# Attention's products with v in four 64x64 quarters of the array

## The chip, the cores and the metric

The kernel is one program on one NeuronCore of a Trainium2 chip. The core has five engines that run beside each other, each with its own queue of instructions: TensorE (matrix products, in the profile PE, and its weight loads, PEld), VectorE (DVE), ScalarE (ACT), GpSimd (POOL) and SyncE (SP, which here mostly issues DMAs). TensorE multiplies a stationary operand, loaded by a weight load, with a moving operand that streams through an array of 128 rows (the contraction, on the partitions of SBUF) and 128 columns (the output's partitions), and writes its result to PSUM, 128 partitions by eight banks of 512 f32. VectorE and ScalarE read PSUM; the next product into a bank waits until they have.

The metric is the device time of one execution in microseconds. The time before is 3694.07 us, the median of three runs (3691.95 to 3695.59).

## The reference, cut to what matters

The reference is a chain of four layers on an image of 48 x 48 positions with 768 channels in f32: a transformer block with global attention, a Fourier mixer, a scan with rotations and depthwise convolutions, and a second Fourier mixer. Only the attention of the first layer is touched by the change:

```python
attn = jnp.einsum('bqc,bkc->bqk', q * scale, k)
...
attn = (attn.reshape(B * nh, H, W, H, W) + rel_h[:, :, :, :, None] + rel_w[:, :, :, None, :]).reshape(B * nh, H * W, H * W)
attn = jax.nn.softmax(attn, axis=-1)
out = jnp.einsum('bqk,bkc->bqc', attn, v)
```

There are 12 heads of 64 channels and 2304 positions. For each head and each query, the scores against all 2304 keys get two position terms, go through the softmax, and weight the rows of v.

## The kernel before

The kernel runs the layers one after another, in stages: normalised input, q, k, v and the position terms (to DRAM); attention; projection; the two-layer perceptron; the first Fourier mixer; the scan; the second mixer. All products are f32, apart from the position terms added to the scores, which are one-pass f32r.

Attention (`attention_bounded`, from line 586) takes the heads in six pairs (`pr`), and each pair's queries in five chunks (`qc`) of 464 columns, the last of 448. A chunk `c = (pr, qc)` goes through the 18 tiles of 128 keys (`kt`), three in a step (`KB = 3`): 6 x 5 x 6 = 180 steps. The two heads of a pair are called `s` = 0 and 1; head `s` has its channels in partitions `64 s` to `64 s + 63`.

For one key tile:

- `products` (line 617) multiplies keys with queries. The contraction is over 64 channels, so head 0 uses the upper 64 rows of the array and head 1 the lower 64, with 128 columns each (the keys). Their results go to two different PSUM banks of one tile `s`; the pool `ps_s` holds three such pairs of banks.
- `scores` (line 626) adds the position terms to the same banks with a one-hot product of 64 rows by 128 columns for each head (line 633), ScalarE takes the exponential of both heads in one instruction into an SBUF tile `p` (line 635), and VectorE adds `p` to an accumulator `acc`, from the second key tile on (lines 640 and 643). No maximum is subtracted: a bound that the first stage computes allows it, and otherwise `attention_any` is run, which the change does not touch.
- `values` (line 647) multiplies v with `p`. The contraction is over the tile's 128 keys, so all 128 rows are used, and each head's 64 channels take one half of the array's columns: 128 rows by 64 columns, the outputs of both heads in the two halves of the partitions of one bank, `av`. It collects over the 18 key tiles.

At the end of a chunk `row_sums` (line 656) multiplies `acc` with a block of ones in the same way, which gives each head's sum over all keys, spread over its 64 partitions, in a bank `rs`; VectorE takes the reciprocal from there. `finish` (line 667) multiplies `av` with it into `oT`, the attention's output in SBUF. `av` and `rs` have one bank each (the pool `ps_v`), so with the six of `ps_s` all eight banks are taken.

The steps overlap by one: in step `i`, `products` and `scores` of step `i` are written first, then `row_sums` (if a chunk ends), `values` and `finish` of step `i - 1`. So at the end of a chunk, the first three key tiles of the next chunk stand on TensorE ahead of the row sums and of the last three products with v, and another three key tiles stand between those and the next chunk's first product into `av`.

Each engine runs its queue in order. The order in a queue is that of the program's text as a priority, but the framework's planner, which simulates the program with its own costs when it is compiled, may put an instruction ahead of another that it expects to be ready later. In the profile the reciprocal (line 664) runs on VectorE ahead of the add of key tile 2 of the next chunk (line 643), which the text has before it.

Beside these, SyncE loads the next keys, values, queries and position terms; GpSimd prepares weights for later stages; and in the first chunk twelve groups of position terms are still computed (`last_terms_w`, line 208: four products of 128 rows by 96 columns each, line 203, then a copy on ScalarE and two subtracts on VectorE). Their PSUM tile has the tag `rs`, too (line 674).

Of the kernel before, what the change touches and what calls it, by code (L numbers as in the profile page):

```python
# [12 lines left out]
F32 = mybir.dt.float32  # L13
F32R = mybir.dt.float32r
AF = mybir.ActivationFunctionType
ALU = mybir.AluOpType
# [4 lines left out]
P = 128  # L21
# [4 lines left out]
NT = T // P  # L26
NH, HD = 12, 64
# [523 lines left out]
def queries(qc):  # L551

    return slice(qc * QB, min(T, (qc + 1) * QB))
# [32 lines left out]
def attention_bounded(tc, ahead, oT, last_terms, beside, load_next):  # L586

    nc = tc.nc  # L600
    KB = 3
    (load_keys_values, load_chunk, load_terms), kvs, qbs, bts, ones, oneh = ahead
    with (
        tc.tile_pool(name="at_p", bufs=10) as pp,
        tc.tile_pool(name="at_r", bufs=2) as rp,
        tc.tile_pool(name="at_o", bufs=2) as op,
        tc.tile_pool(name="at_ps", bufs=3, space=PSUM) as ps_s,
        tc.tile_pool(name="at_pv", bufs=1, space=PSUM) as ps_v,
    ):
        keys = [kv[:, :T] for kv in kvs]  # L610
        vals = [kv[:, T:].rearrange("p (t c) -> p t c", t=NT) for kv in kvs]

        probs, scs = {}, {}
        size = lambda c: queries(c[1]).stop - queries(c[1]).start
        held = lambda c: qbs[(c[0] * NQB + c[1]) % 2]

        def products(c, kt):
            pr, qc = c
            n = size(c)
            ps = ps_s.tile([P, 2, 512], F32, tag="s", name=f"s_{pr}_{qc}_{kt}")  # L620
            for s in range(2):
                rows = slice(s * HD, (s + 1) * HD)
                nc.tensor.matmul(ps[:, s, :n], lhsT=keys[pr % 2][rows, kt * P : (kt + 1) * P], rhs=held(c)[rows, :n], start=True, stop=False)  # L623
            scs[c, kt] = ps

        def scores(c, kt):
            pr, qc = c
            n = size(c)
            b, j = divmod(kt, KJ)
            ps = scs.pop((c, kt))  # L630
            for s in range(2):
                rows = slice(s * HD, s * HD + NBR)
                nc.tensor.matmul(ps[:, s, :n], lhsT=oneh[rows, b % 2, :], rhs=bts[b // 2][rows, j, :n], start=False, stop=True)  # L633
            p = pp.tile([P, 2, QB], F32, tag="p", name=f"p_{pr}_{qc}_{kt}")[:, :, :n]
            nc.scalar.activation(p, ps[:, :, :n], AF.Exp)  # L635
            probs[c, kt] = p

            if kt == 1:
                acc = rp.tile([P, 2, QB], F32, tag="acc", name=f"acc_{pr}_{qc}")[:, :, :n]
                nc.vector.tensor_tensor(acc, probs[c, 0], p, ALU.add)  # L640
                probs[c] = acc
            elif kt > 1:
                nc.vector.tensor_tensor(probs[c], probs[c], p, ALU.add)  # L643

        avs, recs = {}, {}

        def values(c, kt):
            pr, qc = c
            if kt == 0:
                avs[c] = ps_v.tile([P, 512], F32, tag="av", name=f"av_{pr}_{qc}")  # L650
            p = probs.pop((c, kt))
            for s in range(2):
                rows = slice(s * HD, (s + 1) * HD)
                nc.tensor.matmul(avs[c][rows, : size(c)], lhsT=vals[pr % 2][:, kt, rows], rhs=p[:, s, :], start=kt == 0, stop=kt == NT - 1)  # L654

        def row_sums(c):
            pr, qc = c
            n = size(c)
            acc = probs.pop(c)
            rs = ps_v.tile([P, 512], F32, tag="rs", name=f"rs_{pr}_{qc}")  # L660
            for s in range(2):
                nc.tensor.matmul(rs[s * HD : (s + 1) * HD, :n], lhsT=ones, rhs=acc[:, s, :], start=True, stop=True)
            rec = rp.tile([P, QB], F32, tag="rec", name=f"rec_{pr}_{qc}")[:, :n]
            nc.vector.reciprocal(rec, rs[:, :n])
            recs[c] = rec

        def finish(c):
            pr, qc = c
            av, rec = avs.pop(c), recs.pop(c)
            nc.vector.tensor_tensor(oT[:, pr, queries(qc)], av[:, : size(c)], rec, ALU.mult)  # L670

        work = [((pr, qc), k0) for pr in range(NC) for qc in range(NQB) for k0 in range(0, NT, KB)]
        other = beside(op, lambda name: pp.tile([P, 2, QB], F32, tag="p", name=name).rearrange("p a c -> p (a c)")[:, : 2 * TB].rearrange("p (a c) -> p a c", a=2))
        terms = last_terms(rp, lambda name: ps_v.tile([P, 512], F32, tag="rs", name=name))
        other_at = {15 + 28 * n // 5 for n in range(29)}

        def next_terms(c, g):
            if c in sequence:
                load_terms(bts[g], c, g)

        sequence = [(pr, qc) for pr in range(NC) for qc in range(NQB)]
        after = dict(zip(sequence, sequence[1:]))

        mid, end = {2, 3, 4, 5, 7, 8, 9, 10, 11, 13}, {8, 10}
        for i in range(len(work) + 1):
            if i in other_at:
                next(other, None)
            if i == 0:
                next(terms)
            if i == len(work) - 8:  # L690
                load_next()
            if i < len(work):
                c, k0 = work[i]
                pr, qc = c
                nxt = (pr, qc + 1) if qc + 1 < NQB else (pr + 1, 0)
                if k0 == 0 and nxt[0] < NC:
                    load_chunk(held(nxt), nxt)
                if k0 == 0 and c != (0, 0):
                    next_terms(c, NG3 - 1)
                elif k0 in (6, 12):  # L700
                    next_terms(after.get(c), k0 // 6 - 1)
                if k0 == 0 and qc == (1 if pr else 3) and pr + 1 < NC:
                    load_keys_values(kvs[(pr + 1) % 2], pr + 1)
                for kt in range(k0, k0 + KB):
                    products(c, kt)
                    scores(c, kt)
            if i in mid:
                next(terms)
            if i:
                c, k0 = work[i - 1]  # L710
                if k0 + KB == NT:
                    row_sums(c)
                for kt in range(k0, k0 + KB):
                    values(c, kt)
            if i in end:
                next(terms)
            if i:
                if k0 + KB == NT:
                    finish(c)
        for _ in itertools.chain(terms, other):  # L720
            pass
# [663 lines left out]
def block_kernel(ctx: ExitStack, tc: tile.TileContext, a: dict):  # L1385
# [58 lines left out]
    with tc.If(bounded > 0) as which:  # L1444
        attention_bounded(tc, ahead, oT, last_terms, beside, load_pw)
# [489 lines left out]
```

## Time and profile before

| | |
|---|---|
| median of the runs | 3694.07 us |
| profiled execution | 3694.35 us, span 3692.6 us, mean granted clock 0.986 |
| attention | about 494 to 1552 us of the span |
| L654, products with v | 2160 matmul instructions, mean 558 ns each, busy 456.5 us together |
| L623, keys with queries | 2160, mean 566 ns |
| L633, position terms | 1080, mean 729 ns |
| L635, exponential (ScalarE) | 540, mean 940 ns |
| L643, accumulator (VectorE) | 480, mean 1177 ns |
| L664, reciprocal (VectorE) | 30, 3050 ns in the middle |
| L670, output (VectorE) | 30, 627 ns in the middle |

PE is TensorE's matmuls and PEld its weight loads. Matmuls that run beside each other in parts of the array, or that follow each other in its pipeline, overlap in the records, so the mean length of a record is longer than its share of the time; distances between starts say more. Within one line of an answer, "x12" are twelve instructions merged; a bracket at the end of a line is the idle time of the engine ahead of it and what ended that. Shapes of matmuls are given as rows*columns of the weights, and then the moving operand.

### The profile page before, as it was taken

The numbers are of one execution on the slowest core, as the hardware profiler recorded it, in microseconds if no ns is written. First come the engines' busy times: TensorE is split into PE (matmuls) and PEld (weight loads), VectorE is DVE, ScalarE is ACT, GpSimd is POOL, SyncE is SP. The second block draws the span as 40 slices with busy tenths as digits, with TensorE's granted clock in tenths as the row PEclk, the third lists the DMA queues.
The fourth block names the chain that finished last, engine by engine and source line by source line (L and its number), as shares of the span: only waits on it lengthen the run. The fifth ranks groups of instructions, "written<-read, shape, count | busy, mean of one in ns | idle before, by whom it ended". The sixth has DMA issues, their size and how long they took to land.

```text
span 3692.6 us, 52195 instructions
## 1 busy us (share of the span) xinstructions
PE 3592.4 (97%) x20914; PEld 2182.6 (59%) x20914; DVE 1995.3 (54%) x3011; ACT 1140.1 (31%) x1731; POOL 666.3 (18%) x498
## 2 busy tenths in 40 slices
PE   7999989999999999999999999999999998999998
PEld 4666554444444444455555555555568867995685
DVE  6544346666666666655334323232345478994445
ACT  1222134444444444303201210121023265223341
POOL 4010001111111111051000000000023303981131
PEclk9999999999999999999999999999999999999999
DMA  7666764746554543344335433533544302112345
GB/s 254 209 219 191 220 191 127 203 125 160 140 145 118 147 121 102 88 141 157 104 122 171 128 105 121 165 105 107 155 134 111 97 20 101 37 30 83 99 121 154
DMA packets 267738, 491.82 MB, mean 133 GB/s; under 512 B 37182, under 2 KB 220286, under 8 KB 261280
## 3 DMA queue, kind: packets, MB, share of 16 engines
q1 hardware_dynamic: 257680, 467.45, 43.0%
q10 hardware_dynamic: 9808, 20.94, 1.6%
q8 instruction: 168, 2.75, 0.3%
q14 instruction: 82, 0.67, 0.1%
HBM read 344.69 MB, written 143.62 MB: 132 GB/s over the span
## 4 chain that ended last, share of the span: by engine, by line
PE 76%; DVE 3%; POOL 2%; DMA 2%; ACT 1%; issue 1%; ACTq 0%; SPq 0%; DVEq 0%; POOLq 0%
PE p L960 13%; PE p L1023 13%; PE s L623 12%; PE av L654 12%; PE c L1187 4%; PE s L633 3%; PE pj L169 3%; PE f_z L1594 2%; PE f_z L1595 2%; PE f_x L1559 2%; PE so L1365 2%; PE f_u L1609 2%; POOL t L1288 1%; DVE s L1300 1%; DVE H L1284 1%
## 5 line engine op out<-in xcount | busy, mean ns | idle before, releaser
L643 DVE TENSOR_TENSOR acc<-acc,p 128x928 f32<-128x928 f32 (+1 forms) x480 | 565.2, 1177 | 255.2 <-ACT p L635 222.4
L635 ACT ACTIVATE p<-s 128x928 f32<-128x928 f32 (+1 forms) x540 | 506.7, 940 | 522.8 <-PE s L633 501.2
L623 PE MATMUL s<-qt,kv 64*128 64x464 f32 (+1 forms) x2160 | 529.2, 566 | 4.9 <-DMA qt<-q_d 4.9
L1023 PE MATMUL p<-w,h 128*128 128x384 f32 x1512 | 492.7, 486 | 0.0
L654 PE MATMUL av<-p,kv 128*64 128x464 f32 (+1 forms) x2160 | 456.5, 558 | 0.0
L1023 PEld LDWEIGHTS p<-w,h 128*128 128x128 f32 x1512 | 286.2, 190 | 196.9
L633 PE MATMUL s<-bt,oneh 64*128 64x464 f32 (+1 forms) x1080 | 399.1, 729 | 0.9 <-DMA bt<-rh_d 0.9
L623 PEld LDWEIGHTS s<-qt,kv 64*128 64x128 f32 x2160 | 195.4, 187 | 208.0 <-issue 201.7
L960 PE MATMUL p<-x2nT,w 128*128 128x384 f32 x864 | 293.6, 489 | 3.4 <-issue 3.4
L654 PEld LDWEIGHTS av<-p,kv 128*64 128x64 f32 x2160 | 141.9, 137 | 260.5 <-issue 256.7
L355 PE MATMUL qk<-xnT,wqk 128*128 128x384 f32 x756 | 254.0, 493 | 9.2 <-DMA wqk<-wqk_d 9.2
L1280 PE MATMUL c<-H,bands 128*48 128x96 f32 x5632 | 244.0, 247 | 11.4 <-issue 11.0
L1280 PEld LDWEIGHTS c<-H,bands 128*48 128x48 f32 x5632 | 234.4, 123 | 21.2 <-issue 11.4
L960 PEld LDWEIGHTS p<-x2nT,w 128*128 128x128 f32 x864 | 165.3, 191 | 119.3 <-issue 6.0
L960 PE MATMUL p<-xT,w 128*128 128x384 f32 x648 | 220.7, 486 | 0.0
L355 PEld LDWEIGHTS qk<-xnT,wqk 128*128 128x128 f32 x756 | 145.3, 194 | 104.8 <-issue 11.0
L999 POOL TENSOR_TENSOR rr<-rr,ml_b 128x1152 f32<-128x1152 f32 x12 | 33.3, 2776 | 953.6 <-DMA rr<-xr_d 433.0
L955 ACT ACTIVATE h<-h,ml_b 128x384 f32<-128x384 f32 x144 | 88.3, 614 | 346.2 <-DVE h L975 174.3
L1288 POOL TENSOR_TENSOR t<-s,c 128x768 f32<-128x768 f32 x80 | 144.6, 1832 | 182.5 <-DMA bands<-in_bands_dram 171.9
L960 PEld LDWEIGHTS p<-xT,w 128*128 128x128 f32 x648 | 123.1, 190 | 85.9
L633 PEld LDWEIGHTS s<-bt,oneh 64*128 64x128 f32 x1080 | 106.2, 187 | 106.0 <-issue 100.6
L1594 PE MATMUL f_z<-f_w,f_o 97*96 97x96 f32 x800 | 134.5, 250 | 0.0
(323 smaller groups left out, 4677.4 us busy)
## 6 DMA issues: line engine op xcount, KB each, us to landing
w<-w1s_d SPq DMA_DIRECT2D x36, 768.0 KB, 4.2
w<-w2s_d SPq DMA_DIRECT2D x36, 768.0 KB, 4.4
w<-w1s_d SPq DMA_DIRECT2D x36, 576.0 KB, 3.8
w<-in_mlp_w_dram SPq DMA_DIRECT2D x27, 768.0 KB, 4.5
wqk<-wqk_d SPq DMA_DIRECT2D x12, 1344.0 KB, 6.7
yu<-f_ys SPq DMA_DIRECT2D x24, 672.0 KB, 3.8
f_yt<-yu SPq DMA_DIRECT2D x20, 720.0 KB, 6.8
yu<-f_us SPq DMA_DIRECT2D x18, 720.0 KB, 4.5
```

The lines of the kernel that those rows point to most:

```text
L355: nc.tensor.matmul(p[:, :TB], lhsT=w[:, n, c, :], rhs=ops[sb][n][:, c, :], start=c == 0, stop=c == NC2 - 1)
L623: nc.tensor.matmul(ps[:, s, :n], lhsT=keys[pr % 2][rows, kt * P : (kt + 1) * P], rhs=held(c)[rows, :n], start=True, stop=False)
L633: nc.tensor.matmul(ps[:, s, :n], lhsT=oneh[rows, b % 2, :], rhs=bts[b // 2][rows, j, :n], start=False, stop=True)
L635: nc.scalar.activation(p, ps[:, :, :n], AF.Exp)
L643: nc.vector.tensor_tensor(probs[c], probs[c], p, ALU.add)
L654: nc.tensor.matmul(avs[c][rows, : size(c)], lhsT=vals[pr % 2][:, kt, rows], rhs=p[:, s, :], start=kt == 0, stop=kt == NT - 1)
L960: nc.tensor.matmul(p[:, :TB], lhsT=w[n][:, c, :], rhs=rhs[n][:, c, :], start=c == 0, stop=c == NC2 - 1)
L1023: nc.tensor.matmul(ps[t][:, :TB], lhsT=hs[left, f][:, t * P : (t + 1) * P], rhs=wt[:, f % KW2, :], start=f == 0, stop=f == NF2 - 1)
L1187: nc.tensor.matmul(ps[:K, i, :n], lhsT=v[:, c, tok : tok + K], rhs=w[:, cc, c0 : c0 + n], start=cc == NC - 1, stop=cc == 0)
L1280: nc.tensor.matmul(ps[r0 : r0 + G, k // 4, cols], lhsT=bands[:, n - GC, i, :] if gr else bands0[:, n, i, :], rhs=H[:, n, :, d : d + NPR], ...
L1288: GP.tensor_tensor(t, sc[:, ch], c1[:, m0 : m0 + GC].unsqueeze(2).to_broadcast([P, GC, RR, NPR]), ALU.mult)
L1594: nc.tensor.matmul(out, lhsT=o1[:, j, 1:3, :].rearrange("c r h -> c (r h)"), rhs=w2t[:, b, 0, :], start=True, stop=False)
```

## The change

Each product with v is cut along the keys as well. A head's 128 keys of a tile become two halves `k` of 64, each with its own 64x64 quarter of the array: head `s` and half `k` use the rows `64 k` to `64 k + 63` and the columns `64 s` to `64 s + 63`. The two halves of a head write to the same partitions, in two different banks, so `av` becomes a pair of banks, one for each half, and each collects over the 18 key tiles by itself. The row sums are done in the same way.

The two halves are then added. For the row sums ScalarE copies the first bank to `rec`, VectorE adds the second bank and takes the reciprocal in place. For the output ScalarE copies the first bank of `av` to `oT`, VectorE adds the second bank and then multiplies by `rec`, both in place.

`av` now takes both banks of `ps_v`. `rs` and the twelve groups of position terms, which had the other one, take a pair of banks from the three of `ps_s` in turn with the scores.

```diff
+        def quarters():
+            half = lambda n: slice(n * HD, (n + 1) * HD)
+            return ((k, half(k), half(s)) for s in range(2) for k in range(2))
+
         def values(c, kt):
             pr, qc = c
             if kt == 0:
-                avs[c] = ps_v.tile([P, 512], F32, tag="av", name=f"av_{pr}_{qc}")
+                avs[c] = ps_v.tile([P, 2, 512], F32, tag="av", name=f"av_{pr}_{qc}")
             p = probs.pop((c, kt))
-            for s in range(2):
-                rows = slice(s * HD, (s + 1) * HD)
-                nc.tensor.matmul(avs[c][rows, : size(c)], lhsT=vals[pr % 2][:, kt, rows], rhs=p[:, s, :], start=kt == 0, stop=kt == NT - 1)
+            for k, keep, rows in quarters():
+                nc.tensor.matmul(avs[c][rows, k, : size(c)], lhsT=vals[pr % 2][keep, kt, rows], rhs=p[keep, rows.start // HD, :], start=kt == 0, stop=kt == NT - 1)

         def row_sums(c):
             pr, qc = c
             n = size(c)
             acc = probs.pop(c)
-            rs = ps_v.tile([P, 512], F32, tag="rs", name=f"rs_{pr}_{qc}")
-            for s in range(2):
-                nc.tensor.matmul(rs[s * HD : (s + 1) * HD, :n], lhsT=ones, rhs=acc[:, s, :], start=True, stop=True)
+            rs = ps_s.tile([P, 2, 512], F32, tag="s", name=f"rs_{pr}_{qc}")
+            for k, keep, rows in quarters():
+                nc.tensor.matmul(rs[rows, k, :n], lhsT=ones[keep], rhs=acc[keep, rows.start // HD, :], start=True, stop=True)
             rec = rp.tile([P, QB], F32, tag="rec", name=f"rec_{pr}_{qc}")[:, :n]
-            nc.vector.reciprocal(rec, rs[:, :n])
+            nc.scalar.copy(rec, rs[:, 0, :n])
+            nc.vector.tensor_tensor(rec, rs[:, 1, :n], rec, ALU.add)
+            nc.vector.reciprocal(rec, rec)
             recs[c] = rec

         def finish(c):
             pr, qc = c
             av, rec = avs.pop(c), recs.pop(c)
-            nc.vector.tensor_tensor(oT[:, pr, queries(qc)], av[:, : size(c)], rec, ALU.mult)
+            o = oT[:, pr, queries(qc)]
+            nc.scalar.copy(o, av[:, 0, : size(c)])
+            nc.vector.tensor_tensor(o, av[:, 1, : size(c)], o, ALU.add)
+            nc.vector.tensor_tensor(o, o, rec, ALU.mult)
...
-        terms = last_terms(rp, lambda name: ps_v.tile([P, 512], F32, tag="rs", name=name))
+        terms = last_terms(rp, lambda name: ps_s.tile([P, 2, 512], F32, tag="s", name=name)[:, 0])
```

## The prediction, made before the changed kernel had run

> **What bounds the kernel now.** Read first: the page's busy shares, its chain of what ended last, and the attention lines among its costliest groups.
>
> ```profile
> span 3692.6 us, 52195 instructions
> PE 3592.4 (97%) x20914; PEld 2182.6 (59%) x20914; DVE 1995.3 (54%) x3011; ACT 1140.1 (31%) x1731; POOL 666.3 (18%) x498
> ...
> PE p L960 13%; PE p L1023 13%; PE s L623 12%; PE av L654 12%; PE c L1187 4%; PE s L633 3%; PE pj L169 3%; PE f_z L1594 2%; PE f_z L1595 2%; PE f_x L1559 2%; PE so L1365 2%; PE f_u L1609 2%; POOL t L1288 1%; DVE s L1300 1%; DVE H L1284 1%
> ...
> L654 PE MATMUL av<-p,kv 128*64 128x464 f32 (+1 forms) x2160 | 456.5, 558 | 0.0
> ```
>
> TensorE is busy in 97% of the span, and its products with v (L654) are 12% of the chain, with no idle time before them. Attention runs from 494 to 1552 us; in the table by stretch VectorE is busy there for 706 of 1058 us and ScalarE for 513, so neither is the bound. What L654 costs is read from one step of attention, in order of time (weight loads, 700.3 to 706.1 us):
>
> ```profile
> 700.38 0.20 PEld L654 LDWEIGHTS av<-p,kv 128*64 128x64 f32 x4 [0.50 <-issue]
> 700.82 0.14 PEld L654 LDWEIGHTS av<-p,kv 128*64 128x64 f32 x2 [0.25 <-issue]
> 701.21 0.14 PEld L654 LDWEIGHTS av<-p,kv 128*64 128x64 f32 x2 [0.24 <-issue]
> 701.60 0.14 PEld L654 LDWEIGHTS av<-p,kv 128*64 128x64 f32 x2 [0.24 <-issue]
> 701.99 0.14 PEld L654 LDWEIGHTS av<-p,kv 128*64 128x64 f32 x2 [0.24 <-issue]
> 702.86 0.30 PEld L623 LDWEIGHTS s<-qt,kv 64*128 64x128 f32 x4 [0.73 <-issue]
> ...
> 706.03 0.20 PEld L654 LDWEIGHTS av<-p,kv 128*64 128x64 f32 x4 [0.49 <-issue]
> ```
>
> A step (three key tiles) takes 5.65 us. An f32 product appears as two matmul instructions (2160 for 1080 calls). The loads come in twos, 0.39 us apart: the two heads' products run beside each other in the array's two column halves, and a round of two takes 389 ns whatever it loads, because the next weights go in while the present round streams. Six rounds are 2.33 us; the block lasts 2.49 us. The rest is the change of array shape. The last round starts at 702.38 and should end at 702.77, but the load for L623 starts at 702.86, about 97 ns later, and its first round lasts 0.49 us (702.86 to 703.36, the next records' start) in place of 0.39: a pause of some 97 ns and about 104 ns of weight load that nothing covers. On the way into L654 there is the same pause, and the first round lasts 0.44 us: 52 ns of load. About 350 ns a step, 63 us over 180 steps.
>
> Last I read VectorE's order of time where one chunk of queries hands over to the next:
>
> ```profile
> 723.08 1.12 DVE L640 TENSOR_TENSOR acc<-p,p 128x928 f32<-128x928 f32 x1 [3.03 <-ACT p L635]
> 724.12 3.05 DVE L664 RECIPROCAL rec<-rs 128x464 f32<-128x464 f32 x1
> 727.09 1.15 DVE L643 TENSOR_TENSOR acc<-acc,p 128x928 f32<-128x928 f32 x1
> 728.17 0.63 DVE L670 TENSOR_TENSOR oT<-av,rec 128x464 f32<-128x464 f32 x1
> ```
>
> The row sums start on TensorE at 722.98; call that 0. The reciprocal runs from 1.14 to 4.19, L670 frees the `av` bank at 5.82, and the next chunk's first product into `av` starts at 6.43 (729.41). The slack is 0.6 us, and in the hand-over at 1240.03, where GpSimd stretches the add to 1.69 us, it is nothing:
>
> ```profile
> 1246.46 0.20 PEld L654 LDWEIGHTS av<-p,kv 128*64 128x64 f32 x4 [0.50 <-DVE oT L670]
> ```
>
> **The change part by part.**
>
> Array time of the products: 0. Each call becomes two of half the rows, 2160 for 1080, and the row sums 120 for 60. Four quarters of 64x64 fill the same array as two halves of 128x64, each still streams 464 columns, and a key tile still needs two rounds. That rounds of four take 389 ns no row shows; the nearest are L654 (two column halves, 389 ns) and L623 (two row halves into two banks, 389 ns), and a quarter round only crosses them: each row still feeds two streams, each PSUM partition still takes writes into two banks. So 389 ns; the other end is that quarters on the same rows follow one another, +2.33 us a step, +420 us. A gain is excluded here: no column and no pass is saved.
>
> Issue: two tiles of a round start 6.5 ns apart in the single records (700.379 and 700.386), so four end 13 ns later than two. 180 blocks: +2.3 us. The doubled instructions are no limit: the conv's matmuls (L1280) run at 82.5 ns for two loads and two matmuls, 20.6 ns an instruction; a quarter round needs eight in 389 ns.
>
> The change of shape: 0. L623 and L633 use 64 rows x 128 columns, L654 will use 64x64 instead of 128x64, so only the columns differ. The trace has changes of columns alone: from the position terms (L203, all rows, 96 columns) to L654. Their starts lie 178 ns apart in the typical one of ten, 83 ns of streaming and 95 ns of pause, and rows alone (L203 to L623, twice) give 178 too. The pause comes with any change, so I keep it. Ends: all of it kept, 0; all of it gone with the uncovered loads, -63 us.
>
> The Trainium skill ("TensorE: Matmul & The Clock Gate", Part 3) says a weight load overlaps matmuls in flight only when the row group differs. By that, two quarters on the same rows would not hide their loads, and 52 ns would be added to each of six rounds, +56 us. The trace disagrees already: L654's loads start 2 ns after a matmul on the same rows, and the rounds keep 389 ns. I take the row.
>
> Row sums and their bank: `rs` leaves its own bank for the three pairs of the scores. It needs the pair that kt 0 of the next chunk used, whose exponential ended 0.9 us before (at -1.84 + 0.94), and gives it back at about 2.97, while the third key tile of the next step asks at 5.2. 0. The twelve position terms of the first chunk move to the same pairs; ScalarE's copy (0.5 us) and two subtracts of 0.35 us free theirs within some 3.5 us of the step's 6.5 to 7.3. 0; if that cover is gone, 12 waits of at most 0.5 us, +6.
>
> Hand-over on VectorE, now with a copy on ScalarE (0.55 us, the 480-column row L63) ahead of each sum. The `rs` copy starts when kt 2's exponential ends (1.05) and the sums are there (1.14), and is done at 1.7. So the pending accumulator add (kt 2), ready at 1.1, should now go first: 1.29 to 2.42 (dependent adds follow at 1.19 us: three took 3.58 us at 710.81). Then the sum of the two `rs` halves (0.62, as L670) 2.35 to 2.97, the reciprocal 3.03 to 6.08. The `av` copy on ScalarE falls between the end of the values (3.3) and the next exponential (4.58), so no exponential waits for it. The sum of the two `av` halves, queued behind the reciprocal, runs 6.01 to 6.63 and frees the banks; TensorE follows 0.06 us later (as at 1246.40 to 1246.46). It asked at 6.43: it waits 0.26 us. 29 hand-overs, seven of which GpSimd now stretches by some 0.4 us: 22 x 0.25 + 7 x 0.65 = +10 us. Ends: 0 if the `av` sum is placed ahead of the reciprocal; if the reciprocal stays ahead of the kt 2 add, as now, rs sum 1.75, reciprocal 2.43 to 5.48, add to 6.54, `av` sum to 7.09: a wait of 0.7 us, 29 of them +20 us, with GpSimd's share +23.
>
> The multiplication by `rec` now comes after the release and only holds back the next adds, which VectorE catches up within the step (0.6 us against 2 us of idle time before each triple). The end of attention: the last L670 ends at 1551.94; the new chain would end at about 1553.8, and VectorE's next work there starts at 1554.96: 0, at most +2.
>
> Load: VectorE gains 30 x 1.24 = 37 us, ScalarE 60 x 0.55 = 33 us, both beside TensorE.
>
> Sum: 0 + 2.3 + 0 + 0 + 10 + 0 = +12 us. The profiled execution took 3694.35 us (span 3692.6 and 1.75 around it), 0.3 us above the runs' median: 3706.6, and 3707 is what I forecast, with its own range 3697 (issue alone) to 3722 (late reciprocal and the ends above).
>
> **The rivals.**
>
> *The pause goes.* If arrays split by 64 rows on both sides need no drain between them, two pauses a step vanish: 180 x 0.19 = -35 us, net 3672; with the loads covered too -63, net 3644. For it: both shapes now share the row split. Against: the 95 ns at a change of columns alone. It turns the sign once it saves more than 12 / 180 = 67 ns a step.
>
> *Quarters not four at once.* If a round loses the cover of its weight load (52 ns x 6 x 180) it is +56 us, 3763; if quarters follow one another, +420 us, 4127. For it: no row here shows four. Against: the two halves both ways at full rate.
>
> *The reciprocal keeps its place or the copies hold up ScalarE.* 0.7 to 1.2 us a hand-over, +20 to +35 us, 3717 to 3732. For it: the planner now puts the reciprocal ahead of the kt 2 add. Against: its input now comes 0.6 us after that add's.
>
> *The copies are hidden anyway*: the `av` sum goes ahead of the reciprocal, or the reciprocal is quicker from SBUF. +2, 3697.
>
> **How the numbers follow.** A measurement of this kernel tells 0.2%, 7.4 us, from no change. Forecast 55% (3697 to 3722; four fifths of it beyond 7.4 us: slower 0.44, same 0.11); pause gone 13% (faster 0.12, same 0.01); not four at once 14%, slower; late reciprocal 12%, slower; hidden 6%, same. Faster 0.12, same 0.18, slower 0.70. The range leaves out the deep end of the first rival and most of the second: 3668 to 3750.
>
> **What would show it.** L654 with 4320 matmuls whose rounds of four are 389 ns apart, blocks of 2.50 us and steps of 5.66; the pause before L623 still some 97 ns; in the waits L654 behind the `av` sum, some 10 us in all; VectorE's add of kt 2 ahead of the sum of `rs`. The forecast falls if rounds are longer than 389 ns, if the first load of L623 follows the last round without a pause, or if TensorE waits for the score banks (`s`).

## The result

The changed kernel takes 3709.42 us (median of six runs, 3702.25 to 3713.41) against 3693.01 us for the kernel before (six runs, 3689.12 to 3698.63). The ratio is 1.0040, with a 95% interval of 1.0030 to 1.0051: slower by 11 to 19 us, 16.4 by the medians. The forecast was 3707 us, 12 us above the profiled run of before.

The profiled execution has a span of 3707.4 us, 14.8 more than before. From its page, the lines that answer to those read before:

```profile
span 3707.4 us, 56855 instructions
PE 3597.7 (97%) x23194; PEld 2191.3 (59%) x23194; DVE 2042.5 (55%) x3071; ACT 1171.5 (32%) x1791; POOL 666.1 (18%) x498
...
PE 70%; DVE 9%; ACT 3%; DMA 2%; issue 2%; POOL 1%; ACTq 0%; SPq 0%; DVEq 0%; POOLq 0%
...
L659 PE MATMUL av<-p,kv 64*64 64x464 f32 (+1 forms) x4320 | 459.8, 556 | 7.5 <-DVE oT L679 5.9
```

The products with v are now 4320 matmuls of 64 rows and 64 columns, twice as many, and TensorE is busy with them for 459.8 us, as good as before (456.5): four run beside each other where two did. What is new is in the last column: ahead of them TensorE waits for VectorE (line 679 is the sum of the two `av` halves). In the chain of the whole execution VectorE has risen to 9%, from 3%.

One step and the row sums after it, in order of time (weight loads):

```profile
723.07 0.21 PEld L659 LDWEIGHTS av<-p,kv 64*64 64x64 f32 x8 [0.50 <-issue]
723.51 0.15 PEld L659 LDWEIGHTS av<-p,kv 64*64 64x64 f32 x4 [0.24 <-issue]
723.90 0.15 PEld L659 LDWEIGHTS av<-p,kv 64*64 64x64 f32 x4 [0.24 <-issue]
724.29 0.15 PEld L659 LDWEIGHTS av<-p,kv 64*64 64x64 f32 x4 [0.24 <-issue]
724.68 0.15 PEld L659 LDWEIGHTS av<-p,kv 64*64 64x64 f32 x4 [0.24 <-issue]
725.57 0.30 PEld L623 LDWEIGHTS s<-qt,kv 64*128 64x128 f32 x4 [0.73 <-issue]
...
728.73 0.21 PEld L667 LDWEIGHTS rs<-acc,ones 64*64 64x64 f32 x8 [0.50 <-issue]
```

The loads now come in fours, still 0.39 us apart. From the last of them to the first load of L623 it takes 0.89 us, before 0.87: the pause at the change of shape is there as it was. The block takes 2.50 us instead of 2.49.

VectorE at the hand-over that follows; the row sums start at 728.73:

```profile
728.83 1.13 DVE L640 TENSOR_TENSOR acc<-p,p 128x928 f32<-128x928 f32 x1 [3.07 <-ACT p L635]
730.06 1.13 DVE L643 TENSOR_TENSOR acc<-acc,p 128x928 f32<-128x928 f32 x1
731.10 0.63 DVE L670 TENSOR_TENSOR rec<-rs,rec 128x464 f32<-128x464 f32 x1
731.77 3.05 DVE L671 RECIPROCAL rec<-rec 128x464 f32<-128x464 f32 x1
734.75 0.58 DVE L679 TENSOR_TENSOR oT<-av,oT 128x464 f32<-128x464 f32 x1
735.36 1.11 DVE L680 TENSOR_TENSOR oT<-oT,rec 128x464 f32<-128x464 f32 x1
```

And TensorE's next product with v, from its weight loads:

```profile
735.37 0.21 PEld L659 LDWEIGHTS av<-p,kv 64*64 64x64 f32 x8 [0.69 <-DVE oT L679]
```

The add of key tile 2 now goes first, the reciprocal starts at 3.04 after the row sums (before: 1.14), the sum that frees `av` ends at 6.59 (before: 5.82), and TensorE starts at 6.64. It asked at about 6.43.

Where the 14.8 us of the two spans are, by starts of instructions:

| stretch | before | after | difference |
|---|---|---|---|
| up to the first product of attention | 494.55 | 496.75 | +2.2 |
| 29 hand-overs, end of the last chunk's products to the next chunk's first | | | +9.4 |
| blocks of products with v and row sums (176 found whole) | 458.2 | 461.3 | +3.1 |
| rest of attention | | | +1.2 |
| last product of attention to the first of the projection | 0.85 | 2.67 | +1.8 |
| from there to the end | 2141.8 | 2138.9 | -2.9 |

The first and the last row lie outside what was changed. Hand-overs, blocks and the end of attention are 14.3 us. Of the 3.1 us in the blocks, 1.4 lie in a single one, the second of attention, which TensorE enters soon after a wait of over 5 us for data, with a granted clock of 0.50: over the block the clock is 0.71 in the kernel before (517.70 to 521.20) and 0.51 in the changed one (520.77 to 525.60). The changed kernel and the four experiments made from it with three tiles in a step all lose 0.9 to 1.4 us there, the one without quarters too; why is open. The other blocks add 1.7 us. The 1.2 us in the rest of attention were not broken down further.

### The profile page after: what moved, and what is told of

It reads as the page before. It is cut to its first block, busy times and chain, and to the rows that moved or that the text cites. A ratio compares the mean times of both kernels' runs of the same rounds, so it can differ in the third digit from the quotient of the medians.

```text
span 3707.4 us, 56855 instructions
## 1 busy us (share of the span) xinstructions
PE 3597.7 (97%) x23194; PEld 2191.3 (59%) x23194; DVE 2042.5 (55%) x3071; ACT 1171.5 (32%) x1791; POOL 666.1 (18%) x498
## 3 DMA queue, kind: packets, MB, share of 16 engines
q8 instruction: 185, 3.03, 0.3%
## 4 chain that ended last, share of the span: by engine, by line
PE 70%; DVE 9%; ACT 3%; DMA 2%; issue 2%; POOL 1%; ACTq 0%; SPq 0%; DVEq 0%; POOLq 0%
PE p L970 13%; PE p L1033 13%; PE av L659 10%; PE s L623 9%; PE c L1197 4%; PE s L633 2%; PE pj L169 2%; DVE rec L671 2%; PE f_z L1605 2%; PE f_z L1604 2%; PE f_x L1569 2%; PE so L1375 2%; PE f_u L1619 2%; DVE s L1310 2%; DVE H L1294 2%
## 5 line engine op out<-in xcount | busy, mean ns | idle before, releaser
L643 DVE TENSOR_TENSOR acc<-acc,p 128x928 f32<-128x928 f32 (+1 forms) x480 | 571.3, 1190 | 221.3 <-ACT p L635 184.9
L623 PE MATMUL s<-qt,kv 64*128 64x464 f32 (+1 forms) x2160 | 529.4, 566 | 4.7 <-DMA bt<-rw_d 4.7
L659 PE MATMUL av<-p,kv 64*64 64x464 f32 (+1 forms) x4320 | 459.8, 556 | 7.5 <-DVE oT L679 5.9
L623 PEld LDWEIGHTS s<-qt,kv 64*128 64x128 f32 x2160 | 195.8, 187 | 208.4 <-issue 195.8
L659 PEld LDWEIGHTS av<-p,kv 64*64 64x64 f32 x4320 | 150.9, 133 | 263.1 <-issue 239.4
```

The lines of the kernel that those rows point to most:

```text
L659: nc.tensor.matmul(avs[c][rows, k, : size(c)], lhsT=vals[pr % 2][keep, kt, rows], rhs=p[keep, rows.start // HD, :], start=kt == 0, stop=kt ...
```

## The experiments

The theory (A in the expectations): the array does the quarters at no cost but 13 ns of issue per block; the time goes into PSUM that is freed later, `av` at the hand-overs above all. Rival B: the quarters cost the time in the array, with their doubled instructions and loads. Rival C: the copies on ScalarE hold up the exponentials, or VectorE's added work tells. A fourth question is whether the pause at a change of shape was read rightly. Each group of runs has its own runs of the kernel before: 3693.98 us for the first four experiments, 3696.58 for the last three.

| experiment | us | ratio to before, 95% interval |
|---|---|---|
| reciprocal behind the `av` sum | 3699.58 | 1.0016 (1.0007 to 1.0025) |
| one bank read | 3707.33 | 1.0042 (1.0028 to 1.0056) |
| one bank read, row sums copied first | 3702.26 | 1.0013 (1.0004 to 1.0022) |
| the chain behind halves | 3707.80 | 1.0038 (1.0024 to 1.0052) |
| six key tiles in a step, halves | 3666.63 | 0.9925 (0.9911 to 0.9938) |
| six key tiles in a step, quarters | 3666.78 | 0.9919 (0.9906 to 0.9933) |
| keys with queries in quarters | 3849.51 | 1.0415 (1.0399 to 1.0431) |

### The reciprocal behind the sum that frees av

```diff
             nc.vector.tensor_tensor(rec, rs[:, 1, :n], rec, ALU.add)
-            nc.vector.reciprocal(rec, rec)
...
-            nc.vector.tensor_tensor(o, av[:, 1, : size(c)], o, ALU.add)
+            add = nc.vector.tensor_tensor(o, av[:, 1, : size(c)], o, ALU.add)
+            with tc.issue_after(add.ins):
+                nc.vector.reciprocal(rec, rec)
             nc.vector.tensor_tensor(o, o, rec, ALU.mult)
```

> The changed kernel with one order altered: on VectorE the reciprocal is queued behind the sum of the two av halves, which frees the av banks. Theory A (the cost is the later release of av at the 29 hand-overs, 9.4 us in the trace, plus 2.3 us of issue and about 2 us at the end of attention): the sum of the av halves ends at about 4.5 us after the start of the row sums instead of 6.6, TensorE asks at 6.4 and waits no more, and the time falls by some 9 us, to about 3700. Rival B (the quarters themselves cost the time in the array: doubled instructions, loads, rounds): nothing moves, about 3709. Rival C (the copies hold up ScalarE's exponentials, or the added load of VectorE does): nothing moves, about 3709.

3699.58 us, 5.6 above the kernel before. VectorE's order of time at the same hand-over of this kernel, whose row sums start at 728.82 (here line 678 is the `av` sum):

```profile
730.15 1.13 DVE L643 TENSOR_TENSOR acc<-acc,p 128x928 f32<-128x928 f32 x1
731.19 0.63 DVE L670 TENSOR_TENSOR rec<-rs,rec 128x464 f32<-128x464 f32 x1
732.84 0.64 DVE L678 TENSOR_TENSOR oT<-av,oT 128x464 f32<-128x464 f32 x1 [1.01 <-ACT oT L677]
733.39 3.04 DVE L680 RECIPROCAL rec<-rec 128x464 f32<-128x464 f32 x1
```

Nothing is computed less, only the 3 us of the reciprocal have changed places with the sum. `av` is free at 4.7 instead of 6.6 us after the row sums' start. Over the 29 hand-overs the distance from the last product of a chunk to the next chunk's first is that of the kernel before again (-0.02 us in all, +9.4 in the changed kernel). B and C expected 3709 and are out as the main cause. What is left in this trace is 2.7 us in the blocks, 1.5 in the rest of attention and 1.1 at its end. (The profiled execution, 3706.18 us, was the slowest of the eleven of this kernel; some 3.4 us before attention and as many behind it lie outside what was changed.)

### The chain behind halves

The products stay in two column halves, into one bank, and the evacuation is the changed kernel's:

```diff
-            for k, keep, rows in quarters():
-                nc.tensor.matmul(avs[c][rows, k, : size(c)], lhsT=vals[pr % 2][keep, kt, rows], rhs=p[keep, rows.start // HD, :], start=kt == 0, stop=kt == NT - 1)
+            for s in range(2):
+                rows = slice(s * HD, (s + 1) * HD)
+                nc.tensor.matmul(avs[c][rows, 0, : size(c)], lhsT=vals[pr % 2][:, kt, rows], rhs=p[:, s, :], start=kt == 0, stop=kt == NT - 1)
...
-            nc.vector.tensor_tensor(rec, rs[:, 1, :n], rec, ALU.add)
+            nc.vector.tensor_tensor(rec, rs[:, 0, :n], rec, ALU.add)
...
-            nc.vector.tensor_tensor(o, av[:, 1, : size(c)], o, ALU.add)
+            nc.vector.tensor_tensor(o, av[:, 0, : size(c)], o, ALU.add)
```

> The kernel before with its products in two column halves, but with the changed kernel's work behind them: row sums in a pair of the score banks, copy on ScalarE, add, reciprocal, and for the output copy, add and multiplication; the same bank is added to its copy both times, so both the sums and the output double and the quotient stays. Theory A: hand-over waits of 9 us and about 2 us at the end come without any quarter, about 3704. Rival B: 3693, as before. Rival C: about 3704.

3707.8 us, 13.8 above the kernel before, without a single quarter. Its waits of the weight loads (here line 660 is the product with v, 680 the second addition into the output):

```profile
PEld av L660 <- DVE oT L680: 23.9, 27, 2.1
```

About 0.5 us of idle time stands before these loads in any case (in the kernel before, the row at 700.38 has 0.50 with nothing to wait for); what is beyond it is the wait. Measured against the kernel before, the 29 hand-overs are 10.5 us longer, and the end of attention 1.8 us. The evacuation alone, without the quarters, loses as much as the change does, as far as these runs can tell (interval 9 to 19 us).

### One bank read

```diff
-            nc.scalar.copy(rec, rs[:, 0, :n])
-            nc.vector.tensor_tensor(rec, rs[:, 1, :n], rec, ALU.add)
-            nc.vector.reciprocal(rec, rec)
+            nc.vector.reciprocal(rec, rs[:, 0, :n])
...
-            nc.scalar.copy(o, av[:, 0, : size(c)])
-            nc.vector.tensor_tensor(o, av[:, 1, : size(c)], o, ALU.add)
-            nc.vector.tensor_tensor(o, o, rec, ALU.mult)
+            nc.vector.tensor_tensor(o, av[:, 0, : size(c)], rec, ALU.mult)
```

> The changed kernel without the sums of the halves: all products in quarters and into two banks as in the change, but the reciprocal is taken from the first bank of the row sums and the output is made from the first bank of av, as the kernel before did with its one bank; the second banks are not read, so half of the keys is left out of the output. Theory A: the release of av is back at 5.8 us, no waits; only the issue of four quarters instead of two is left, +2.3 us on the kernel before, about 3696. Rival B: the array work is all there, about 3709. Rival C: no copies, about 3696.

This kernel leaves half of the keys out of its sums and its output; the array does all the work of the change. It takes 3707.33 us: the expectation of theory A, 3696, was missed by 11 us, and B's was met. The trace shows why that is no case for B. TensorE's weight loads in this kernel:

```profile
732.40 0.30 PEld L623 LDWEIGHTS s<-qt,kv 64*128 64x128 f32 x4 [0.52 <-DVE rec L669]
...
733.59 0.21 PEld L659 LDWEIGHTS av<-p,kv 64*64 64x64 f32 x8 [0.50 <-DVE oT L676]
```

The reciprocal has lost its place ahead of the key tile 2 add (729.30, the row sums having started at 726.93), and it now reads a pair of the score banks, which it holds for its whole 3.05 us, until 5.42 after the row sums. The third key tile of the next step asks for that pair at about 5.2, and all 29 hand-overs are longer by 0.2 us or more, 11.7 us together. I had taken away the chain and put a new wait in its place, at another pair of banks. So I ran it once more with the reciprocal taken from a copy:

```diff
-            nc.vector.reciprocal(rec, rs[:, 0, :n])
+            nc.scalar.copy(rec, rs[:, 0, :n])
+            nc.vector.reciprocal(rec, rec)
```

> The changed kernel again without the sums of the halves (second banks not read, half of the keys left out), but with the first bank of the row sums copied by ScalarE and the reciprocal taken from that copy in SBUF, so that the pair of score banks is free again at about 1.7 us after the start of the row sums. In the run without the copy the pair was held until the reciprocal had ended (5.4 us), and the third key tile of the next step waited for it. Theory A (late releases of PSUM are the cost, the quarters are not): no wait for the pair, the output frees av at about 6.1 us, TensorE asks at 6.4 and does not wait; the kernel before plus 2.3 us of issue and about 2 us at the end of attention, 3697 to 3699. Rival B (the quarters cost the time in the array): 3707 to 3709 as before.

3702.26 us beside 3696.58, 5.7 more (interval 1.5 to 8); theory A expected 3 to 5, B 13 to 15. VectorE at a hand-over whose row sums start at 725.86:

```profile
728.23 3.05 DVE L670 RECIPROCAL rec<-rec 128x464 f32<-128x464 f32 x1
731.37 0.64 DVE L677 TENSOR_TENSOR oT<-av,rec 128x464 f32<-128x464 f32 x1
```

The output's multiplication frees `av` at 6.15, and TensorE asks at 6.4. The wait for the score banks is gone, and 2.6 us of waits for `av` remain, in the few hand-overs in which GpSimd stretches VectorE's add. So the whole array work of the change, with both of its banks, is there in this run at about a third of the loss.

### Six key tiles in a step

```diff
-    KB = 3
+    KB = 6
...
-        tc.tile_pool(name="at_p", bufs=10) as pp,
+        tc.tile_pool(name="at_p", bufs=13) as pp,
...
-        other_at = {15 + 28 * n // 5 for n in range(29)}
+        other_at = {8 + 14 * n // 5 for n in range(29)}
...
-        mid, end = {2, 3, 4, 5, 7, 8, 9, 10, 11, 13}, {8, 10}
+        mid, end = {1, 2, 3, 4, 5, 6}, {1, 2, 3, 4, 5, 6}
...
-            if i == len(work) - 8:
+            if i == len(work) - 4:
```

> The kernel before, with six key tiles in a step instead of three (13 buffers for the exponentials instead of 10, the side work's places in the steps halved), so that the array changes its shape half as often. My reading of the step (two pauses of about 97 ns and 52 and 104 ns of uncovered weight load at the two changes of shape, 350 ns): 90 x 0.35 = 31 us less, about 3662. Rival: the gaps belong to the waits for data of a block and not to the change of shape, or the 13 buffers are too few and ScalarE waits: no gain, 3693 or slower.

> The changed kernel with six key tiles in a step (13 buffers for the exponentials), beside the kernel before with six tiles, which took 3667. With six tiles some 5.9 us of scores stand between the last product with v of a chunk and the next chunk's first, instead of 3.2, so the release of av at 6.6 us is early enough. Theory A: no waits at the hand-overs; the quarters cost 1.2 us of issue (90 blocks) and about 2 us at the end, 3668 to 3671. Rival B (quarters cost in the array, whatever stands around them): 14 to 16 us over the six-tile kernel, 3681 to 3683.

The kernel before with six tiles takes 3666.63 us, a ratio of 0.9925: 23 to 33 us less, where 31 were expected from half as many changes of shape. So the gaps come once for each turn of the products with v and not with each tile. That it is the change of shape that makes them, and not a block's first wait, this run alone does not show; the keys in quarters, below, add changes of shape without new waits for data. The end of such a block in its weight loads:

```profile
704.49 0.14 PEld L654 LDWEIGHTS av<-p,kv 128*64 128x64 f32 x2 [0.24 <-issue]
704.88 0.14 PEld L654 LDWEIGHTS av<-p,kv 128*64 128x64 f32 x2 [0.24 <-issue]
705.75 0.30 PEld L623 LDWEIGHTS s<-qt,kv 64*128 64x128 f32 x4 [0.73 <-issue]
```

The rounds and the gap of 0.87 us are those of three tiles; there are half as many gaps.

With quarters on top it takes 3666.78, beside 3696.58 in its own group of runs: not to be told from the halves. With twice the work between two chunks, the later release of `av` is early enough: no product with v waits for the `av` sum in its trace, and the 29 hand-overs take 193.1 us, with halves 193.4. Between the first product of keys with queries and the last product with v the traces have 1026.2 us for halves and 1027.6 for quarters, and 1.8 us more at the end of attention for quarters: the 1.2 and 2 us that were expected. Both kernels beat the two compared in this study.

### Keys with queries in quarters

```diff
-                nc.tensor.matmul(ps[:, s, :n], lhsT=keys[pr % 2][rows, kt * P : (kt + 1) * P], rhs=held(c)[rows, :n], start=True, stop=False)
+                for m in range(2):
+                    cols = slice(m * HD, (m + 1) * HD)
+                    nc.tensor.matmul(ps[cols, s, :n], lhsT=keys[pr % 2][rows, kt * P + m * HD : kt * P + (m + 1) * HD], rhs=held(c)[rows, :n], start=True, stop=False)
```

> The kernel before, with the products of keys and queries in 64x64 quarters too (each head's 128 keys in two column halves), while the position terms stay in 64 rows by 128 columns and the products with v in 128 rows by 64 columns. So each key tile now has a change of columns alone, on the same row split, into the position terms and out of them. If a change of columns alone costs the same pause as any other (my reading: 97 ns, with 104 ns of uncovered load for 128 columns and 52 for 64), each of 540 key tiles gains one change into the position terms (201 ns, of which some 15 are paid now) and 360 gain one out of them (149 ns): 540 x 0.19 + 360 x 0.15 = 155 us, less 52 ns of shorter load at 180 block starts, 9 us: about 3840. Rival (no pause where both sides split the rows by 64, which would also have made the change faster): loads are covered and nothing is drained, 3694 or a few us less.

3849.51 us beside 3696.58: 153 us more, 146 expected. Two key tiles in its weight loads (here line 625 is keys with queries, 635 the position terms):

```profile
703.85 0.21 PEld L625 LDWEIGHTS s<-qt,kv 64*64 64x64 f32 x8 [0.70 <-issue]
704.76 0.19 PEld L635 LDWEIGHTS s<-bt,oneh 64*128 64x128 f32 x2 [0.70 <-issue]
705.16 0.21 PEld L625 LDWEIGHTS s<-qt,kv 64*64 64x64 f32 x8 [0.22 <-issue]
706.07 0.19 PEld L635 LDWEIGHTS s<-bt,oneh 64*128 64x128 f32 x2 [0.70 <-issue]
```

These rows lie in a chunk of 448 columns. Two key tiles of such a chunk in the kernel before:

```profile
675.14 0.40 PEld L623 LDWEIGHTS s<-qt,kv 64*128 64x128 f32 x4 [0.18 <-issue]
...
676.09 0.41 PEld L623 LDWEIGHTS s<-qt,kv 64*128 64x128 f32 x4 [0.18 <-issue]
```

A key tile takes 1.31 us (703.85 to 705.16), against 0.95 with one shape; in the chunks of 464 columns it is 1.35 against 0.99. Both shapes split the rows by 64, and going from one to the other costs 0.36 us for a change into and one out of the position terms, as much as the two changes of shape in a step of the kernel before (0.35). So the rival by which the pause would go has nothing for it.

All of attention in 64x64 quarters, position terms too, would need no change of shape at all. That wasn't tried.

## Why the prediction was right

The forecast was 12.3 us, and 11 to 19 were measured, 16.4 by the medians. The price was put on the right step, the release of `av` at the hand-overs; how near the sum came is in part luck, as said below.

- **Array time, 0.** Right. Rounds of four are 0.39 us apart. The rival "quarters not four at once" is out: TensorE's busy time on the line rose by 3.3 us in all, where that rival had 56 or 420, and with six tiles the quarters cost nothing that the runs can tell.
- **Issue, +2.3.** Right, a little high: the typical block is 10 ns longer, for 13 forecast, 1.7 us in all. The other 1.4 us of the blocks are the one block at a low clock, which the sum did not have.
- **Change of shape, 0.** Right, in the trace (0.89 us against 0.87) and by the run with keys and queries in quarters. (The L203 matmuls that the prediction reads at 83 ns start 85 ns apart in most cases, so its pause of 95 ns is one of 93.)
- **Weight loads.** The Trainium skill's rule ("TensorE: Matmul & The Clock Gate", Part 3), by which two quarters on the same rows would not hide their loads, 56 us by the prediction's estimate, does not hold here: in the changed kernel too, the loads start 2 ns after a matmul on the same rows (723.514 after 723.512), and the rounds keep 389 ns.
- **Bank of the row sums, 0.** Right within attention: no wait for a score pair shows at the hand-overs. (At the end of attention it may have cost something, see below.) How near it was, the one-bank run shows: its third key tile asked at about 5.2, as worked out, and a pair held until 5.42 made every hand-over wait. Which pair is held, and how long, was worth the line it had.
- **Hand-over, +10.** Measured +9.4. The order on VectorE came as foreseen, the key tile 2 add ahead of the sum of `rs`, the reciprocal at 3.04 (forecast 3.03), the `av` sum done at 6.59 (6.63), since it took 0.58 us and not 0.62. The prediction's 1.19 us from add to add was a misreading (the three adds at 710.81 start 1.23 us apart), which shifts the chain by 0.04 us. A typical hand-over waits 0.21 us (0.26 forecast), and two of the 29 do not wait. GpSimd's share was put at seven hand-overs of 0.65 us, 4.6 us; it was five, of 0.5 to 1.3 us, 4.7 us. That two misses, in the number and in the length, cancel here is luck.
- **End of attention, 0, at most +2.** The mis-sized term: it cost 1.8 us. The prediction compared the new end of VectorE's chain with VectorE's own next work and overlooked TensorE, whose first projection product does not read the last chunk's output and yet waits. In the changed kernel's weight loads:

```profile
1565.43 0.15 PEld L659 LDWEIGHTS av<-p,kv 64*64 64x64 f32 x4 [0.22 <-issue]
1568.46 0.62 PEld L169 LDWEIGHTS pj<-pw,oT 128*128 128x128 f32 x3 [2.88 <-issue]
```

In the single records TensorE's sequencer waits there for a count of VectorE's, and goes on 40 ns after the reciprocal has ended (1568.35); with the reciprocal put last, 40 ns after the `av` sum. Which dependency the count stands for was not settled; a PSUM bank that the projection takes over is the nearest guess. It would fit that the distance from the last product with v to the projection is 0.47 to 1.33 us in the three kernels whose row sums keep their own bank (the kernel before, its six tiles, its keys in quarters) and 1.96 to 2.67 us in the six that have them in a score pair; then the cost would belong to the bank of the row sums. With six tiles and quarters, though, TensorE goes on 0.39 us after the `av` sum, where no VectorE instruction ends, so this is not shown.

Added up by the trace, 9.4 + 1.7 + 1.8 = 12.9 us stand against 12.3, and 14.3 with the block at a low clock.

## What to carry to other kernels

Splitting a contraction that already fills the rows makes no column less to stream; it only buys a second bank to empty, so price it by what empties the banks and by who waits for them. At a hand-over put the instruction that frees PSUM ahead of long work that nobody waits for: moving a 3 us reciprocal behind a 0.6 us sum won back two thirds of the loss (5.6 us instead of 16.4). When matmuls of two shapes take turns, count the turns: here each pair of changes costs 0.35 us (0.30 by the whole time of the run with half as many), and longer turns were worth more than anything else in this study.

## What the runs showed of the hardware that was not expected

- Whether GpSimd's work stretched a VectorE instruction went by where its operands lay. Adds of two SBUF operands took up to 1.97 us instead of 1.13 in attention (L643 before; each of the stretched ones ran beside a GpSimd instruction), and the multiplication of two SBUF operands once 1.11 instead of 0.64 (L680 after). Those with one operand in PSUM stayed within 0.02 us over all 30 chunks, though five of L670's and four of L679's ran beside GpSimd (after), and so did the reciprocal from SBUF for the same number of columns (3.05 us, five of 30 beside GpSimd). The sum of the `av` halves, with its PSUM operand, was not stretched; the adds queued ahead of it were.
- The reciprocal took the same from SBUF as from PSUM, 3.05 us for 464 columns, 6.6 ns a column, five times an add.
